# Two graph layers on one core: PSUM pools in another order, one operation for row plus normed row, index work queued later, and both extra weight places opened with the last projection

## The chip, the cores and the metric

The kernel runs on one core of a Trainium2 chip. A core has five engines, each with an instruction stream of its own: TensorE (matrix products; PE in the profile, with its weight loads as PEld), the vector engine (DVE), the scalar engine (ACT), GpSimd (POOL) and SyncE (SP). In this kernel SP issues the loads of weights (and a few small transfers early on); ACT and POOL issue nearly all others. All transfers run on the core's 16 DMA engines. The metric is the device time of one execution in microseconds (us). The times of three runs of the kernel before are 1063.53, 1063.5 and 1066.45 us, the median is 1063.53.

## The reference

The input is 384 nodes with 1024 features and 12288 edges. Layer 0 is graph attention plus a mixing layer plus an expert layer that routes each node to two of eight experts; layer 1 is a graph aggregation plus linear attention plus an expert layer that routes each node to one of eight experts. The change lies from the last projection of layer 1 on; what is computed there is:

```python
x = x + gnn(xn) + mix(xn)                 # mix ends in a projection, a residual, a norm
feats = layernorm(x)
aff = feats @ centroids.T
eid = argmax(aff, axis=1)                 # one expert for each node
xhat = (feats - mean) * rsqrt(var + eps)
for e in range(8):
    h = xhat * gamma[e] + beta[e]
    y = feats + relu(h @ w1[e] + b1[e]) @ w2[e] + b2[e]
    alpha = sigmoid(feats @ centroids[e])
    out = out + mask_e * (alpha * y + (1 - alpha) * feats)
x = x + out
```

Since alpha * feats and (1 - alpha) * feats add up to feats, a node's result is x + feats + alpha * (relu(h @ w1 + b1) @ w2 + b2), all of the one expert of that node.

## The kernel before

**Tiling.** The 384 nodes are three blocks of 128 partitions (`nb`); the 1024 features are eight chunks of 128 (`kc`) or two halves of 512 (`hf`). All numbers are 32-bit floats. A weight place holds 2048 KB (16 KB in each partition): one half of a 1024 x 1024 matrix, or all of one expert's w1 or w2 in layer 1.

**Order.** The kernel is written with a tile framework: pools of tiles with a fixed number of buffers, and a scheduler that orders each engine's instructions by its own estimate and sets the waits. Pools that are closed give their memory to later ones, and the first user of a new tile then waits for the last users of what lay there. `tc.issue_after(i)` queues what is issued inside it, on the engine of `i`, behind `i`.

**Weights.** `load_w` and `load_t` (L104 to L125) take the next place from a list called `ring` and issue the load on SP. The list begins as the pool `w` with three places; layer 0 adds one (`w_top`, L606) and two (`w_more`, L727). `layer1` puts one place of the pool `w_last` in front of the list (`LAST`, L37) when the pool `mid` is closed, just ahead of the last projection; `experts1_sorted` appends one place of the pool `w_end`. So the last stretch runs on eight places, as many as two pairs of experts need. SP works its queue in order: a load whose place isn't free yet holds up all that stand behind it.

**The last projection and the router (`layer1`, L1105 to L1215).** `project` multiplies the attention output with `w_fc` (L1116), `mix_norm` norms it and adds it to `x`. `to_router(nb)` transposes the row block into `xT` (L215, L216), multiplies with the centroids (L1150), takes the moments of the row and norms it twice: the expert input goes to `xn1`, half on DVE and half on ACT (`norm_on_both`), and `norm_on_act` (L186) writes the normed row `ft` on ACT (L190). `to_places(nb)` picks the expert, finds the node's place among that expert's rows (`place`), and scatters the row to `xg` in DRAM (L291 on POOL). POOL then adds `ft` to `x` for the first two blocks (L1186), DVE for the third (L1214). `to_first` builds the first expert pair's rows, transposed, as a product with a one-hot matrix (L1190); `scaled` (L967) applies that pair's gamma and beta, the first half on DVE (L973, L974), the second on ACT (L980), giving `xe0`. Last, ACT computes alpha (`info`), and POOL scatters alpha and node number to `ig` (L291).

**The experts (`experts1_sorted`, L1293 to L1382).** The experts go in four pairs, 64 places for each. For a pair: `rows_of` transposes the loaded rows `xs` (L1317) and scales them into `xeT`; `hidden_of` is the w1 product (L1326), whose result DVE and ACT copy to `hs` (L1329, L1330); `by_feature` transposes it (L1338) and adds the bias with relu, half on DVE (L1346), half on ACT (L1344); `give` is the w2 product (L1357), scaled by alpha on DVE (L1360) and scattered with an addition to `out` (L291). The first pair's rows are `xe0`; the other pairs' rows come back from `xg` (L1308). `inf` (L1367) is alpha and node number by place; `half` (L1372) makes the row numbers for the scatters of it; b2 is gathered by node (L306), and L1374 adds alpha * b2 to `x`, which ACT then stores to `out` (L1376). The scatters into `out` wait for these three stores. PSUM has eight banks: `layer1` has four in the pool `pm` and then four in `px`; `experts1_sorted` opens four for transposes (`ps_t4`), then two for h and two for y.

Of the kernel before, what the change touches and what calls it, by code (L numbers as in the profile page):

```python
# [10 lines left out]
F32 = mybir.dt.float32  # L11
I32 = mybir.dt.int32
AF = mybir.ActivationFunctionType
OP = mybir.AluOpType
# [22 lines left out]
LAST = 1  # L37
# [7 lines left out]
def gps_two_layers(ctx: ExitStack, tc: tile.TileContext, d, out: bass.AP):  # L45
# [140 lines left out]
    def norm_on_act(dst, src, mean, rinv):  # L186

        off = small.tile([P, 1], F32, tag="off", name="off")
        ve.tensor_scalar(off, mean, rinv, -1.0, op0=OP.mult, op1=OP.mult)
        ac.activation(dst, src, AF.Identity, bias=off, scale=rinv)  # L190
# [696 lines left out]
    def experts0_sorted(keep):  # L887

        slots, share = keep["slots"], keep["share"]
        with tc.tile_pool(name="act6", bufs=1) as act, \  # L890
                tc.tile_pool(name="work6", bufs=2) as work, \
                tc.tile_pool(name="ps_t6", bufs=3, space=PSUM) as pt, \
                tc.tile_pool(name="ps_h6", bufs=5, space=PSUM) as ph:
# [73 lines left out]
    def scaled(dst, src, g, es):  # L967

        if g == 0:
# [4 lines left out]
            ve.tensor_tensor(to, to, bt, OP.add)  # L974
            return
# [6 lines left out]
    def layer1(keep=None):  # L982


        with tc.tile_pool(name="act2", bufs=1) as act, \
                tc.tile_pool(name="work3", bufs=2) as work, \
# [5 lines left out]
            ed_w = part.tile([P, NB, N], F32, name="ed_w")  # L992
# [3 lines left out]
            hn = act.tile([P, NB, KC * K2V], F32, tag="rows3", name="hn")  # L996
# [40 lines left out]
            kn = act.tile([P, NB, D], F32, tag="kq", name="kn")  # L1037
# [31 lines left out]
            vn = act.tile([P, NB, KC * K2V], F32, tag="rows3", name="vn")  # L1069
# [6 lines left out]
            kv = part.tile([P, KC, K2V], F32, name="kv")  # L1076
# [11 lines left out]
            qT = act.tile([P, KC, N], F32, tag="kq", name="qT2")  # L1088
# [48 lines left out]
            ft = act.tile([P, NB, KC * K2V], F32, tag="rows3", name="ft4")  # L1137
            xT = act.tile([P, KC, N], F32, tag="kq", name="xT4")
# [5 lines left out]
            def to_router(nb):  # L1144
                mix_norm(nb)
                xs, xb, fb = x[:, nb, :], xn1[:, nb, :], ft[:, nb, :D]
                to_t(pm, xT, xs, nb)
                ps = px.tile([P, HB], F32, tag="x", name="x")
                for kc in range(KC):
                    mm(ps[:, :X], lhsT=xT[:, kc, nb * P:(nb + 1) * P], rhs=cen[:, kc, :],  # L1150
# [13 lines left out]
                norm_on_act(fb, xs, mean, rinv)  # L1164
                sums[nb] = (ps, less, rinv)

            def to_places(nb):
                xb, fb = xn1[:, nb, :], ft[:, nb, :D]
# [15 lines left out]
                if nb < NB - 1:  # L1184
                    with tc.issue_after(last[0].ins):
                        gp.tensor_tensor(x[:, nb, :], x[:, nb, :], fb, OP.add)  # L1186
# [27 lines left out]
            ve.tensor_tensor(x[:, NB - 1, :], x[:, NB - 1, :], ft[:, NB - 1, :D], OP.add)  # L1214
# [78 lines left out]
    def experts1_sorted(xe0):  # L1293

        with tc.tile_pool(name="w_end", bufs=1) as w_end, \
                tc.tile_pool(name="act4", bufs=1) as act, \
# [197 lines left out]
```

## Time and profile before

| | us |
|---|---|
| median of the runs | 1063.53 |
| the profiled execution's own time | 1067.88 |
| its span | 1066.2 |
| TensorE busy | 1017.0 (95%) |
| DVE busy | 350.4 (33%) |
| ACT busy | 269.7 (25%) |
| POOL busy | 321.9 (30%) |
| TensorE busy in the window from 980 to 1000 | 14.78 of 20 |
| end of the last y product | 1057.5 |

The span is what the profiler saw from the first to the last instruction; the execution's own time has 1.7 us around it. In the lines of a timeline the first column is the start, the second the time from the first to the last instruction of a merged group (or the duration of a single one); "x32" counts instructions, and each product of 32-bit floats is recorded as two. The brackets hold the idle time of the engine just before the group, and what ended it. Lines of windows give the length, then each engine's busy time with the count of its instructions, then the granted clock of TensorE (1.00 is full), the mean busy share of the 16 DMA engines, and GB/s.

### The profile page before, as it was taken

Reading aid. Unit: us, or ns where it says so; the run is one execution under the profiler, and the core shown is the slowest. Engines: PE = TensorE matmul, PEld = TensorE weight load, DVE = VectorE, ACT = ScalarE, POOL = GpSimd, SP = SyncE. Lnnn points to the kernel's source line nnn. Section 1 sums busy time; section 2 is a strip of 40 time slices with the busy share of each in tenths; the row PEclk is TensorE's granted clock in tenths of the full one; section 3 lists DMA queues with packets and bytes.
Section 4 is the critical chain, followed back from the end, with each engine's and each line's share of the span. In section 5 each row is a group of like instructions: output and inputs, shape, how many; then the busy total and the mean of one; then the engine's idle time right before and its main releaser. Section 6 shows DMA issues by size and latency. Waiting matters only on the chain. (4 is left out here: it accounts for less than half of the span.)

```text
span 1066.2 us, 9480 instructions
## 1 busy us (share of the span) xinstructions
PE 1017.0 (95%) x3437; PEld 554.8 (52%) x3437; DVE 350.4 (33%) x973; ACT 269.7 (25%) x499; POOL 321.9 (30%) x277
## 2 busy tenths in 40 slices
PE   6999999999999999999998999959999999998895
PEld 4555555544555555544465665424444465555252
DVE  4580000006667766701342110061306000474221
ACT  3111111110876666611131111221302010122120
POOL 2142466566686778500001000130002000013121
PEclk9999999999999999999998999969999999998998
DMA  9939523334425242532365888968522222425994
GB/s 348 401 127 372 146 80 103 135 113 93 77 1 138 22 78 1 159 110 98 113 216 210 300 314 289 393 233 293 197 79 79 79 79 79 158 79 197 388 383 120
DMA packets 69813, 183.35 MB, mean 172 GB/s; under 512 B 21520, under 2 KB 22384, under 8 KB 69504
## 3 DMA queue, kind: packets, MB, share of 16 engines
q1 hardware_dynamic: 40640, 146.01, 38.2%
q0 software_dynamic: 25120, 28.88, 11.6%
q10 hardware_dynamic: 4000, 7.79, 1.9%
q8 instruction: 29, 0.48, 0.2%
q14 instruction: 24, 0.20, 0.1%
HBM read 160.22 MB, written 22.96 MB: 172 GB/s over the span
## 5 line engine op out<-in xcount | busy, mean ns | idle before, releaser
L479 POOL DMA_INDIRECT countd<-seen,cells x96 | 153.2, 1596 | 63.2 <-DMA countd<-seen,cells 38.0
L134 PE MATMUL mm<-xnT,w 128*128 128x384 f32 x512 | 165.7, 486 | 0.0
L665 PE MATMUL mm<-xnT,w 128*128 128x384 f32 x384 | 132.4, 493 | 0.0
L134 PEld LDWEIGHTS mm<-xnT,w 128*128 128x128 f32 x512 | 97.1, 190 | 67.5 <-DVE xnT L216 0.2
L479 POOL DMA_INDIRECT lastd<-typ,cells x96 | 95.1, 991 | 110.0 <-DMA lastd<-typ,cells 70.3
L665 PEld LDWEIGHTS mm<-xnT,w 128*128 128x128 f32 x384 | 70.5, 190 | 56.4 <-issue 13.4
L713 PE MATMUL mm<-w,t 128*128 128x512 f32 x192 | 84.3, 595 | 0.8 <-DVE x L401 0.8
L146 PE MATMUL mm<-w,xnT 128*128 128x512 f32 x192 | 82.8, 592 | 0.0
L134 PE MATMUL mm<-t,w 128*128 128x384 f32 x256 | 82.7, 486 | 0.0
L915 PE MATMUL h<-w,xeT 128*128 128x352 f32 x224 | 68.3, 462 | 0.7 <-DVE xeT L907 0.3
L134 PEld LDWEIGHTS mm<-t,w 128*128 128x128 f32 x256 | 48.6, 190 | 33.9
L146 PEld LDWEIGHTS mm<-w,xnT 128*128 128x128 f32 x192 | 36.3, 190 | 45.5 <-issue 45.5
L713 PEld LDWEIGHTS mm<-w,t 128*128 128x128 f32 x192 | 35.9, 190 | 44.1 <-issue 42.2
L585 DVE TENSOR_TENSOR kind<-last 128x1152 f32<-128x1152 f32 x1 | 1.4, 1359 | 165.3 <-DMA last<-lastd 165.3
L915 PEld LDWEIGHTS h<-w,xeT 128*128 128x128 f32 x224 | 41.9, 190 | 24.4 <-DVE xeT L907 2.4
L291 POOL DMA_INDIRECT xg<-xn,slot x3 | 4.0, 1341 | 140.6 <-DVE xn L1127 135.5
L1011 PE MATMUL mm<-w,xnT 128*128 128x512 f32 x96 | 44.8, 627 | 1.3 <-DVE xnT L216 1.3
L1116 PE MATMUL mm<-w,oT 128*128 128x512 f32 x96 | 42.6, 595 | 0.0
L942 PE MATMUL y<-w,hT 128*128 128x512 f32 (+1 forms) x96 | 41.6, 592 | 0.0
L146 PE MATMUL mm<-w,t 128*128 128x512 f32 x96 | 41.4, 592 | 0.0
L526 ACT ACTIVATE t<-mm,cols 128x384 f32<-128x384 f32 x24 | 13.9, 580 | 106.5 <-PE mm L134 106.5
L1066 POOL TENSOR_TENSOR x<-x,gb 128x1024 f32<-128x1024 f32 x3 | 7.3, 2425 | 101.2 <-DVE x L1065 101.2
(298 smaller groups left out, 1201.6 us busy)
## 6 DMA issues: line engine op xcount, KB each, us to landing
w<-in_w1s SPq DMA_DIRECT2D x16, 1408.0 KB
w<-in_xw SPq DMA_DIRECT2D x8, 2048.0 KB
w<-in_xw2s SPq DMA_DIRECT2D x8, 2048.0 KB
w<-in_w2s SPq DMA_DIRECT2D x8, 1536.0 KB
keys<-keyd POOLq DMA_DIRECT2D x4, 1536.0 KB
xg<-blank SPq DMA_DIRECT2D x12, 512.0 KB
xs<-xg POOLq DMA_DIRECT2D x10, 512.0 KB
w<-in_wk SPq DMA_DIRECT2D x2, 2048.0 KB
```

Source lines behind the costliest of these rows:

```text
L134: mm(ps[:, :N], lhsT=w[:, j, kc, :], rhs=rhs[:, kc, :], start=kc == 0, stop=kc == KC - 1)
L146: mm(ps, lhsT=lhs[:, kc, nb * P:(nb + 1) * P], rhs=w[:, kc, :], start=i == 0 and kc == 0, stop=i == len(pairs) - 1 and kc == KC - 1)
L291: i = gp.indirect_dma_start(rows, bass.IndirectOffsetOnAxis(ap=at, axis=0), src, None, bounds_check=n - 1, oob_is_err=False, compute_op=op)
L479: gp.indirect_dma_start(cells[:, :], bass.IndirectOffsetOnAxis(ap=at[:, i, c:c + 1], axis=0), src[:, c:c + 1], None, bounds_check=N * N + ...
L526: ac.activation(dst[:, ob, :], ps, AF.Identity, bias=cols[:, i, ob:ob + 1], scale=1.0)
L665: mm(ps[:, :N], lhsT=w[:, j, kc, :], rhs=xnT[:, kc, :], start=kc == 0, stop=kc == KC - 1)
L713: mm(pss[hf], lhsT=src[:, kc, nb * P:(nb + 1) * P], rhs=w_out[("mwo", "wo")[part]][hf][:, kc, :], start=part == 0 and kc == 0, stop=part = ...
L915: mm(ag[i][:, :F0], lhsT=xeT[kc // 4][:, kc % 4, :], rhs=w1[kc // 4][:, kc % 4, i * F0:(i + 1) * F0], start=kc == 0, stop=kc == KC - 1)
L942: mm(y, lhsT=hT[:k, e, j, :], rhs=w2[:k, e % 2 * len(K2) + j, :], start=j == 0, stop=j == len(K2) - 1)
L1011: mm(ps, lhsT=xnT[:, kc, nb * P:(nb + 1) * P], rhs=ws[hf][:, kc, :], start=kc == 0, stop=kc == KC - 1)
L1066: gp.tensor_tensor(x[:, b, :], x[:, b, :], gb[:, 1, :], OP.add)
L1116: mm(ps, lhsT=oT[:, kc, nb * P:(nb + 1) * P], rhs=ws[hf][:, kc, :], start=kc == 0, stop=kc == KC - 1)
```

## The change

- The three PSUM pools of `experts1_sorted` are opened in the order h, y, transposes; the two of `experts0_sorted` in the order h, transposes.
- `norm_on_act`, which wrote the normed row into `ft`, becomes `add_normed`: x * (rinv + 1) + off in place, on ACT. `ft` goes, and with it the additions on POOL and DVE.
- `hn`, `kn`, `vn` and `qT` move to the pool `mid`; `kv` shares a buffer with `ed_w`; `xT` becomes a tile of one block from the pool `work`, which gets three buffers.
- `LAST` is 2: both extra places are opened with the last projection; `w_end` goes.
- `half`, the three L1374 and the stores of `out` are queued behind the scaling of pair 1's rows, which are now transposed before the first pair's w2 product; the stores move from ACT's queue to SP's.

```diff
-LAST = 1
+LAST = 2
...
-    def norm_on_act(dst, src, mean, rinv):
+    def add_normed(x, mean, rinv):
         off = small.tile([P, 1], F32, tag="off", name="off")
         ve.tensor_scalar(off, mean, rinv, -1.0, op0=OP.mult, op1=OP.mult)
-        ac.activation(dst, src, AF.Identity, bias=off, scale=rinv)
+        more = small.tile([P, 1], F32, tag="more", name="more")
+        ve.tensor_scalar(more, rinv, 1.0, None, op0=OP.add)
+        ac.activation(x, x, AF.Identity, bias=off, scale=more)
...
-                tc.tile_pool(name="ps_t6", bufs=3, space=PSUM) as pt, \
-                tc.tile_pool(name="ps_h6", bufs=5, space=PSUM) as ph:
+                tc.tile_pool(name="ps_h6", bufs=5, space=PSUM) as ph, \
+                tc.tile_pool(name="ps_t6", bufs=3, space=PSUM) as pt:
...
-                tc.tile_pool(name="work3", bufs=2) as work, \
+                tc.tile_pool(name="work3", bufs=3) as work, \
...
-            hn = act.tile([P, NB, KC * K2V], F32, tag="rows3", name="hn")
+            hn = part.tile([P, NB, KC * K2V], F32, tag="rows3", name="hn")
...
-            kn = act.tile([P, NB, D], F32, tag="kq", name="kn")
+            kn = part.tile([P, NB, D], F32, tag="kq", name="kn")
...
-            kv = part.tile([P, KC, K2V], F32, name="kv")
+            kv = part.tile([P, NB * N], F32, tag="ed", name="kv")[:, :KC * K2V].rearrange("p (k c) -> p k c", c=K2V)
...
-                to_t(pm, xT, xs, nb)
+                xT = work.tile([P, D], F32, tag="xn", name="xT4").rearrange("p (a b) -> p a b", b=P)
+                to_t(pm, xT, xs, 0)
...
-                norm_on_act(fb, xs, mean, rinv)
+                add_normed(xs, mean, rinv)
...
-                if nb < NB - 1:
-                    with tc.issue_after(last[0].ins):
-                        gp.tensor_tensor(x[:, nb, :], x[:, nb, :], fb, OP.add)
...
-            ve.tensor_tensor(x[:, NB - 1, :], x[:, NB - 1, :], ft[:, NB - 1, :D], OP.add)
...
-        with tc.tile_pool(name="w_end", bufs=1) as w_end, \
-                tc.tile_pool(name="act4", bufs=1) as act, \
+        with tc.tile_pool(name="act4", bufs=1) as act, \
                 tc.tile_pool(name="work5", bufs=2) as work, \
-                tc.tile_pool(name="ps_t4", bufs=4, space=PSUM) as pt, \
                 tc.tile_pool(name="ps_h4", bufs=2, space=PSUM) as ph, \
-                tc.tile_pool(name="ps_y4", bufs=2, space=PSUM) as py:
-            ring.append(w_end)
+                tc.tile_pool(name="ps_y4", bufs=2, space=PSUM) as py, \
+                tc.tile_pool(name="ps_t4", bufs=4, space=PSUM) as pt:
...
-                    if hf == 0 and between is not None:
-                        got = rows_of(between)
-                return got if between is not None else None
...
-            for hf in range(2):
-                ve.tensor_scalar(half[:, hf, :], inf[:, :, 1].bitcast(I32), 2.0, float(hf), op0=OP.mult, op1=OP.add)
-            for nb in range(NB):
-                ve.scalar_tensor_tensor(x[:, nb, :], b2[:, nb, :], keep["info"][:, nb, 0:1], x[:, nb, :],
-                                        op0=OP.mult, op1=OP.add)
-                ac.dma_start(out[nb * P:(nb + 1) * P, :], x[:, nb, :])
-            xeT = give(0, by_feature(0, hs), 1)
+            hT = by_feature(0, hs)
+            xeT = rows_of(1)
+            with tc.issue_after(scaled_by[0].ins):
+                for hf in range(2):
+                    ve.tensor_scalar(half[:, hf, :], inf[:, :, 1].bitcast(I32), 2.0, float(hf), op0=OP.mult, op1=OP.add)
+                for nb in range(NB):
+                    ve.scalar_tensor_tensor(x[:, nb, :], b2[:, nb, :], keep["info"][:, nb, 0:1], x[:, nb, :],
+                                            op0=OP.mult, op1=OP.add)
+                    nc.sync.dma_start(out[nb * P:(nb + 1) * P, :], x[:, nb, :])
+            give(0, hT)
```

## The prediction

> **What bounds the kernel now.** TensorE is busy for 1017.0 of 1066.2 us, so I read the timeline of TensorE first, for the places where it waits, and only then what it waits for. The change touches the stretch from the last projection of layer 1 to the end, and there it waits like this:
>
> ```profile
> 975.35 3.47 PE L1190 MATMUL first<-own,xn 128*128 128x128 f32 x16 [1.18 <-DVE slot L1181]
> 981.38 8.78 PE L1326 MATMUL h<-w,xe 128*64 128x512 f32 x32 [2.56 <-ACT xe L980]
> 994.00 0.84 PE L1338 MATMUL t<-ident,hs 128*128 128x128 f32 x4 [3.84 <-issue]
> 1005.53 7.09 PE L1326 MATMUL h<-w,xeT 128*64 128x512 f32 x32 [0.83 <-DVE xeT L974]
> 1045.79 0.84 PE L1338 MATMUL t<-ident,hs 128*128 128x128 f32 x4 [0.59 <-DVE hs L1329]
> 1050.46 7.05 PE L1357 MATMUL y<-w,hT 128*64 128x512 f32 x28 [1.85 <-SPq L1392]
> ```
>
> Call the hidden product of expert pair p h0..h3 (L1326), the output product y0..y3 (L1357), the two w1 loads of a pair A0a, A0b.., the two w2 loads B0a, B0b... h0 starts 2.56 us late and takes 8.78 where h1 takes 7.09; then 3.84 us of nothing; then three even pairs of 16 us; and y3 waits for a weight (its releaser is put down to SP's queue). Now the weight queue (second column: from the first issue to the end of the last of the group) and the 16 DMA engines (windows: PE, PEld, DVE, ACT, POOL busy, clock, DMA share, GB/s):
>
> ```profile
> 963.67 16.37 SPq L123 DMA_DIRECT2D w<-in_xw2s  x2
> 990.19 0.92 SPq L123 DMA_DIRECT2D w<-in_xw  x2
> 1004.73 1.07 SPq L123 DMA_DIRECT2D w<-in_xw2s  x2
> 1012.64 2.71 SPq L123 DMA_DIRECT2D w<-in_xw  x2
> 1021.47 7.84 SPq L123 DMA_DIRECT2D w<-in_xw2s  x2
> ```
>
> ```profile
> 974.00:976.00 2.00, 0.82 (x4) 0.72 (x5) 1.42 (x10) 1.99 (x3) 0.00 (x0) 0.50 0.00 0
> 980.00:982.00 2.00, 0.62 (x4) 0.25 (x6) 0.00 (x0) 1.33 (x5) 1.70 (x4) 0.94 0.66 78
> 982.00:984.00 2.00, 2.00 (x8) 0.68 (x6) 0.00 (x0) 0.00 (x0) 1.07 (x2) 0.50 0.87 252
> 1006.00:1010.00 4.00, 4.00 (x22) 1.42 (x20) 0.14 (x1) 0.53 (x2) 0.00 (x0) 1.00 1.02 419
> 1035.00:1040.00 5.00, 5.00 (x26) 2.32 (x24) 1.50 (x2) 0.00 (x0) 2.14 (x2) 1.00 1.02 410
> ```
>
> B1a goes out at 963.67; B1b, the second of that group, only at about 979.67, since its place lies in memory that L1214 and the row scatters still use. From 982 to 1044 no window has a DMA share below 0.87. So the end is set by the weight stream: it empties at 1050.46, and y3's 7.05 us and the 8.7 us from 1057.52 to 1066.2 follow. TensorE's own work is second, some 2.8 us behind (1.85 and about 0.9 inside y3's first four).
>
> The index work, on the vector engine and GpSimd:
>
> ```profile
> 978.06 1.22 DVE L1214 TENSOR_TENSOR x<-x,ft 128x1024 f32<-128x1024 f32 x1
> 979.20 0.69 DVE L974 TENSOR_TENSOR xe<-xe,gbx 128x512 f32<-128x512 f32 x1
> 993.33 0.24 DVE L1372 TENSOR_SCALAR half<-inf 128x4 int32<-128x4 int32 x2 [13.45 <-DMA b<-in_b,own_e]
> 1002.93 1.28 DVE L1374 SCALAR_TENSOR_TENSOR x<-b,info,x 128x1024 f32<-128x1024 f32 x1 [1.58 <-DMA b<-in_b,own_e]
> ```
>
> ```profile
> 988.19 0.77 POOL L1367 DMA_DIRECT2D inf<-ig x1 [5.12 <-DMA ig<-info,slot]
> 1012.13 1.63 POOL L291 DMA_INDIRECT out<-o,half x1 [19.17 <-DMA out<-x]
> ```
>
> `half` stands before the copy of h0 on the vector engine and waits for `inf`: that is the 3.84 us.
>
> **The change, part by part.** *PSUM order in experts1_sorted.* h0's bank was one of px's, still read by L980 to 981.33; now it is one of pm's, long free, and in the built program h0 waits only for L974; its second half waits for L980 piece by piece. L974 also loses L1214 in front of it: 978.06 + 0.69 = 978.75. h0 starts at 978.9, 2.5 us earlier, with no idle in front, so I take 7.1 us for it (row 1005.53), bound 8.78: it ends at 986.0 instead of 990.16. *PSUM order in experts0_sorted*: no wait of TensorE changes in the built program; 0.
>
> *Row plus normed row in one.* Two POOL additions (2.37 us each, beside the projection) and L1214 go; the ACT operation keeps its 1.23 us; three small vector operations of 0.15 us come. The last stands before the last place, where the vector engine waits 0.68 us for the rank: 0 to 0.15, I take 0.1, on the chain to 975.35.
>
> *Index work later.* `half` and the three L1374 stand behind the scaling of pair 1. The copy of h0 needs no `inf`: the wait becomes 0.6 (row 1045.79), 3.2 us less. Pair 1's eight transposes (1.8 us) move from inside y0 to before it. So y0 starts at 986.0 + 0.6 + 0.9 + 2.0 = 989.5 and ends at 997.3 (7.1 to 8.2 long); h1 starts at 997.4 instead of 1005.53: 8.1 us.
>
> *Two places with the last projection, none at the end.* Eight places as before, but both of the last ones come free when the last L1097 and DVE reader of the middle tiles are done, about 914. The first four loads go out at the same four releases (840.10, 860.70, 886.70, 907.34), then A0a and A0b at about 914 instead of one of them; all are read from 978.9 on, so nothing of that shows. The gain: B1a and B1b now take the two places of w_fc, free at 953.7 and 963.67. B1b leaves the full stretch. *Tiles moved into the middle pool, a third work buffer*: the only wait removed is 0.78 us of POOL at 708, for rows that TensorE reads 30 us later; 0.
>
> *The stores of `out`* move from ACT's queue to SP's, between A2a and A2b. Behind them in SP's line are A2b, B2, A3, B3: each waits until L1374 has run three times, which waits for the third b2 gather.
>
> **The sum.** TensorE alone would gain 8.1 + 2.8 = 10.9 us. It doesn't get it, because the stream binds. From 982 to 1050 the windows carry 24.7 MB, nine of the 2.10 MB loads among it. One of them goes: 2.10 / 0.417 MB per us (windows from 1004 to 1015) = 5.0 us. Against it, nothing but the pair rows can run before A2a: they are issued at 981.4 as before and I let them start at 983, where the stream of before had moved about 0.25 MB already: 0.6 us. The other bound is the stream's start with B1b, about 981.2: 1.8 us. So 3.2 to 5.0, I take 4.4, since the row 980 to 982 has only 78 GB/s at a share of 0.66: the small index scatters hold the engines there, and B1b got little. These scatters now run without a load beside them; `inf` then follows at about 983.5 instead of 988.19 (bound: 988.19), the b2 gathers at 984.5 to 988.
>
> Does SP's line run dry? Pair rows, b2, A2a and the stores are 6.8 MB from 983 on: 16.8 us, to 999.8. A2b goes out behind the third L1374: after pair 1's scaling (990.6), after half and two L1374 and the first half of y0 (994), and after the third gather, about 996 (1.57 MB beside A2a at half the rate), so at 997.8, first bytes 1.6 us later (estimate, from the 963.67 load and its bytes in the window from 964). That fits by 0.4 us. If the third gather takes the 11 us it took in before (991.96 to 1002.93), A2b is at 1000 and 1.7 us are lost: bounds 0 and 1.7, I take 0, since one load competes with it instead of two.
>
> TensorE will wait about 5 us before h3 and 1 to 2 before y3. After 2.56 us of waiting the clock fell to 0.50 and h0 lost 1.7; after 1.85 before y3 it stayed 1.00. A loss in h3 is hidden by y3's wait; in y3 it counts: bounds 0 and 1.7, I take 0, by the row at the same place.
>
> The Trainium skill (TensorE: Matmul & The Clock Gate, section Part 1: The HAM clock gate) speaks against this: an idle window of about 3.4 us halves the clock until about as long a busy one has passed. The two falls in the trace, after 2.56 and 3.84 us, fit such free-running windows; by the rule a longer wait at y3 would cost up to 1.7, an estimate, and the sum would be 2.7 instead of 4.4.
>
> So 4.4 us: span 1061.8, time of the profiled execution 1067.88 - 4.4 = 1063.5. That execution lies 4.35 above the median of the runs, 1063.53; against the median I predict 1059.1.
>
> **Rivals.** *The stream does not bind* outside a profiled execution (the plain runs are 4.35 us faster, which speaks for it; full windows at 410 to 419 speak against): TensorE's 10.9 us come, 1052.6. *The freed load does not shorten the stream*: it starts later by the full 1.8 us and loses 1.7 at A2b, 5.0 - 3.5 = 1.5 us, 1062. *Slower: the stores block SP.* If the third gather lands when it did before, at 1002.93, the third store goes at 1004.3, A2b at 1004.7 instead of 990.7, first bytes at 1006.3 while the stream was empty from 999.8: 6.5 us lost against 4.4 won, 1065.6. It decides from a landing of about 1001 on, and is beyond 0.3% from 1004. For it: a weight load behind a store on one queue is new. Against: two loads and a late `inf` made that landing, and both go.
>
> **How the numbers follow.** 0.3%, 3.2 us, is what a measurement here can tell from no change. Forecast 0.62 (own range 1057 to 1061; 0.54 faster, 0.08 same), stream not binding 0.12 (faster), no shorter stream 0.12 (same), blocked SP 0.14 (0.12 slower, 0.02 same). Faster 0.66, same 0.22, slower 0.12. The range 1054.5 to 1063.5 takes in the forecast, the second rival and the near part of the first, and leaves out 0.08 of the first and 0.12 of the slower one.
>
> **What would show it.** h0 at 979 with no wait, 7.1 long at clock 1.00; the transposes of h0 0.6 us after it; h1 at 997 to 998; B1b at 963.7; `inf` near 983.5; the stores at 993 to 997, A2b right behind; waits of some 5 us before h3 and 1 to 2 before y3; the stream empty near 1046. Wrong if A2b comes after 1001, if a window between 983 and 1040 shows the engines idle, or if y3 starts at half clock.

## The result and the profile after

The changed kernel takes 1065.25 us (median of 14 executions, 1059.32 to 1066.74) beside 1066.53 us for the kernel before (median of 14, 1063.28 to 1069.32). The ratio is 0.9982 with a 95% interval of 0.9968 to 0.9997, a gain of 1.9 us (0.3 to 3.4); the two medians lie 1.3 us apart. Within what a measurement here tells from no change, that is "same". The forecast was 1059.1 with a range of 1054.5 to 1063.5.

The first trace of the changed kernel is of an execution of 1059.32 us, its shortest of all. Its TensorE timeline, to be held against the lines of before (start, length, line, shapes, idle time ahead of it):

```profile
971.30 3.78 PE L1187 MATMUL first<-own,xn 128*128 128x128 f32 x16 [1.38 <-DVE slot L1181]
975.01 8.19 PE L1324 MATMUL h<-w,xe 128*64 128x512 f32 x32
983.76 0.84 PE L1336 MATMUL t<-ident,hs 128*128 128x128 f32 x4 [0.56 <-issue]
992.32 7.04 PE L1324 MATMUL h<-w,xeT 128*64 128x512 f32 x32
...
1029.21 10.09 PE L1324 MATMUL h<-w,xeT 128*64 128x512 f32 x30 [3.05 <-SPq L1390]
...
1040.78 8.27 PE L1355 MATMUL y<-w,hT 128*64 128x512 f32 x32
```

h0 has no wait ahead of it, the 3.84 us behind it are 0.56, and a new wait of 3.05 us stands ahead of most of h3. But the first line alone is 4.05 us earlier than in the first trace of before (975.35), in a part that the change hardly touches. So I measure everything from the start of this product, the third of the tile `first`, called S. The time from S to the end of the span, the end stretch, is 86.3 us in this trace and was 90.85 before: 4.5 us, about what I forecast, and more than the medians show. The queue of weights on SP, where the stores (L1374 here) now stand between A2a and A2b, in the same trace:

```profile
950.57 9.90 SPq L123 DMA_DIRECT2D w<-in_xw2s  x2
983.23 0.37 SPq L123 DMA_DIRECT2D w<-in_xw  x1
987.86 5.79 SPq L1374 DMA_DIRECT2D out<-x  x3
993.74 0.53 SPq L123 DMA_DIRECT2D w<-in_xw  x1
```

B1b is out by 960.5, before the full stretch. A2b goes out at 993.74, which is S + 22.4, and the windows around the danger point (S + 24 to S + 30; DMA share and GB/s are the last two columns) are full:

```profile
995.30:997.30 2.00, 2.00 (x12) 0.72 (x10) 0.00 (x0) 0.00 (x0) 0.00 (x0) 1.00 1.03 416
997.30:999.30 2.00, 2.00 (x11) 0.44 (x7) 0.00 (x0) 0.00 (x0) 0.00 (x0) 1.00 1.02 412
999.30:1001.30 2.00, 2.00 (x17) 1.67 (x16) 1.74 (x4) 1.25 (x4) 1.45 (x1) 1.00 0.99 358
```

Had I stopped here, I would have called the forecast right and the medians noise. The other traces say otherwise.

### The profile page after: what moved, and what is told of

It is laid out like the page before. It is cut to its first block, busy times and chain, and to the rows that moved or that the text cites. A ratio compares the mean times of both kernels' runs of the same rounds, so it can differ in the third digit from the quotient of the medians.

```text
span 1057.6 us, 9480 instructions
## 1 busy us (share of the span) xinstructions
PE 1012.9 (96%) x3437; PEld 551.8 (52%) x3437; DVE 348.5 (33%) x975; ACT 270.2 (26%) x499; POOL 318.4 (30%) x275
## 3 DMA queue, kind: packets, MB, share of 16 engines
q0 software_dynamic: 25120, 28.88, 11.9%
## 5 line engine op out<-in xcount | busy, mean ns | idle before, releaser
L667 PEld LDWEIGHTS mm<-xnT,w 128*128 128x128 f32 x384 | 70.5, 190 | 56.4 <-issue 13.4
L917 PEld LDWEIGHTS h<-w,xeT 128*128 128x128 f32 x224 | 41.9, 190 | 24.5 <-DVE xeT L909 2.5
```

What stands on the lines that cost most here:

```text
L667: mm(ps[:, :N], lhsT=w[:, j, kc, :], rhs=xnT[:, kc, :], start=kc == 0, stop=kc == KC - 1)
L917: mm(ag[i][:, :F0], lhsT=xeT[kc // 4][:, kc % 4, :], rhs=w1[kc // 4][:, kc % 4, i * F0:(i + 1) * F0], start=kc == 0, stop=kc == KC - 1)
```

## The experiments

### More traces of the two kernels

Edit: none. These are further executions of the two kernels.

> The changed kernel once more, for a second trace of it. Its profiled execution so far ended 1.55 us ahead of its own start-of-stretch mark by 86.3 us and was 5.7 us below its median, while before's was 1.4 above. If the stretch from the start of the third `first` product to the end is 86 to 87 again, the change gains 4 us or more at the end and what differs between runs lies in the first 970 us. If it is 88 to 90, the first trace was a lucky one: then the length of the wait ahead of h3 and the windows at half clock behind it vary from run to run, and that is where the gain goes.

(In the first trace the stretch from the mark to the end was 86.3 us.)

> The kernel before once more, for a second trace. Its end stretch, from the start of the third `first` product to the end of the span, was 90.85 us. Theory G (the change gains 3.4 to 4.5 us at the end of every execution, and what hides a part of it in the medians is how the clock's idle windows fall in two earlier places, at 568 and 710 us, that cost 0 to 5.3 us): it is 90 to 92 again. Rival H (the first trace of before had a long end and most executions a shorter one): it is 88 to 89.5.

> The changed kernel a third time. Its end stretch was 86.3 and 87.5 us, in two executions that both lie 4 to 6 us below its median and both lost little at 568 and 710 us. Theory G: 86 to 88 again, and if this execution lies near the median, it is the start of the third `first` product that comes at 974 to 977 instead of 971.3. Rival H: an execution near the median has that start at about 971.4 and an end stretch of 90 or more.

> The kernel before, third trace. In two traces y3's last 28 records took 7.05 us at clock 1.00, behind waits of 1.85 and 2.26 us, and the end stretch was 90.85 and 90.2 us. If y3 at half clock belongs to the changed kernel (its stalls ahead of h3 and y3 are longer), it is 7.05 again and the stretch 90 to 91. If it is a matter of where the clock's windows happen to lie, it may be 8 to 8.8 here too, and the stretch 92.

> The changed kernel, fourth trace. Where h0 runs at full clock (7.1 us), A2a goes out 10.7 us after the start of the third `first` product, ahead of the b2 gathers' bytes, and I expect the third L1372 at 23 to 25 us, A2b at 25, windows with a share below 0.9 between 24 and 30 us, and the end of the stream at 69.5 to 71. Where h0 runs partly at half clock (8.2 us), A2a goes out at 11.9, A2b at 22 to 24, no dry window, and the stream ends at 68 to 69. The end stretch is 18 us more than the stream's end, and 20 where y3 runs at half clock.

Measured: the 12 executions of after_again have a median of 1065.05 us and a ratio to before of 0.9989 (0.9974 to 1.0005), a gain of 1.2 us whose interval takes in zero. The traces follow, with those of the experiments below in the same table. Times are from S, except S, h0 and y3; "last weight" is the start of y3's last 28 records, which the last load (B3b) releases (where no wait is recorded, marked ~, the end of y3 less 7.05 us); "y3" is the length of those 28.

| trace | S | h0 | third L1372/L1374 ends | A2b out | last weight | y3 | end stretch |
|---|---|---|---|---|---|---|---|
| before | 975.35 | 8.78 | 28.9 | with A2a | 75.1 | 7.05 | 90.85 |
| before_again | 974.34 | 10.02 | 27.0 | with A2a | 74.5 | 7.05 | 90.2 |
| before_third | 974.38 | 10.01 | 27.3 | with A2a | 74.4 | 7.05 | 89.9 |
| after | 971.30 | 8.19 | 22.0 | 22.4 | ~70.7 | | 86.3 |
| after_again | 971.42 | 8.17 | 23.1 | 23.6 | 71.9 | 7.05 | 87.5 |
| after_third | 976.00 | 7.09 | 24.7 | 25.1 | 73.9 | 8.75 | 91.3 |
| after_fourth | 975.11 | 7.09 | 25.0 | 25.4 | 72.8 | 7.05 | 88.5 |
| e1_places | 974.42 | 8.78 | 21.0 | with A2a | 72.7 | 7.05 | 88.3 |
| e2_order | 972.95 | 7.09 | 29.8 | 30.2 | 77.8 | 8.75 | 95.0 |
| e6_order_act | 974.68 | 7.09 | 31.2 | with A2a | ~75.3 | | 90.9 |
| e4_act_stores | 975.54 | 7.09 | 24.5 | with A2a | 70.6 | 7.05 | 86.3 |
| e4_again | 975.70 | 7.09 | 24.3 | with A2a | ~70.5 | | 86.2 |
| e8_gather_first | 975.98 | 7.09 | 17.7 | 18.1 | 71.1 | 8.75 | 88.4 |

The mean end stretch is 90.3 us before and 88.4 after: 1.9 us, as the first ratio has it. That the two agree so well is partly luck: of the four executions of the changed kernel two are among its shortest (1059.32 and 1060.68 us), and after_third, at 1068.98, is longer than all others. So neither of my two theories was right as put: the change does not gain 3.4 to 4.5 us in every execution (G), and the first trace of before was no long one (H). The changed kernel's end stretch differs by 5 us between executions, before's by 1. The fourth trace, whose h0 took 7.09 us, came as its expectation has it for A2a (S + 10.7), the third L1372, A2b and the windows (0.61 from S + 24 to S + 26). The third trace shows where the time goes. Its vector engine, with the three L1372 that wait for the gathers of b2:

```profile
994.26 1.29 DVE L1372 SCALAR_TENSOR_TENSOR x<-b,info,x 128x1024 f32<-128x1024 f32 x1 [3.85 <-DMA b<-in_b,own_e]
996.98 1.28 DVE L1372 SCALAR_TENSOR_TENSOR x<-b,info,x 128x1024 f32<-128x1024 f32 x1 [1.43 <-DMA b<-in_b,own_e]
...
999.37 1.28 DVE L1372 SCALAR_TENSOR_TENSOR x<-b,info,x 128x1024 f32<-128x1024 f32 x1 [0.45 <-DMA b<-in_b,own_e]
```

The third gather of b2, which the last of these waits for, was issued at 988.91, 10.5 us earlier. Its line, and below it the same pair in the first trace, 8.1 us apart:

```profile
988.91 1.00 POOL L308 DMA_INDIRECT b<-in_b,own_e  x1 [0.30 <-issue]
```

```profile
983.89 1.00 POOL L308 DMA_INDIRECT b<-in_b,own_e  x1 [0.30 <-issue]
```

```profile
992.00 1.28 DVE L1372 SCALAR_TENSOR_TENSOR x<-b,info,x 128x1024 f32<-128x1024 f32 x1 [1.25 <-DMA b<-in_b,own_e]
```

The SP queue of the third trace, its windows (the clock is the number ahead of the DMA share) and its TensorE timeline:

```profile
986.73 0.37 SPq L123 DMA_DIRECT2D w<-in_xw  x1
995.58 5.44 SPq L1374 DMA_DIRECT2D out<-x  x3
1001.11 1.28 SPq L123 DMA_DIRECT2D w<-in_xw  x1
```

```profile
1000.00:1002.00 2.00, 2.00 (x12) 0.72 (x10) 1.32 (x2) 0.00 (x0) 0.00 (x0) 1.00 0.64 250
1002.00:1004.00 2.00, 2.00 (x16) 1.21 (x12) 0.94 (x2) 0.45 (x2) 0.00 (x0) 1.00 0.76 240
1004.00:1006.00 2.00, 2.00 (x11) 1.00 (x11) 1.60 (x6) 2.00 (x8) 1.09 (x1) 1.00 0.95 332
...
1051.50:1054.50 3.00, 3.00 (x9) 0.88 (x7) 0.00 (x0) 0.00 (x0) 0.00 (x0) 0.50 0.02 5
```

```profile
979.63 7.09 PE L1324 MATMUL h<-w,xe 128*64 128x512 f32 x32
...
1026.99 8.32 PE L1355 MATMUL y<-w,hT 128*64 128x512 f32 x29 [4.05 <-DMA w<-in_xw2s]
...
1049.90 8.75 PE L1355 MATMUL y<-w,hT 128*64 128x512 f32 x28 [2.31 <-SPq L1390]
```

The third store goes at 1001, A2b behind it at 1001.11 (S + 25.1), and the DMA engines run partly dry for 6 us: against 415 GB/s the three windows lack 0.33, 0.35 and 0.17 MB, which is 2.0 us of stream. TensorE then waits 4.05 us in y2 and 2.31 in y3, and y3 falls to half clock on top (0.50 from 1051.5 to 1054.5).

### The places alone, and the order alone

e1_places (the lines of L1293 to L1382 of before that order the index work, and both orders of the PSUM pools, put back):

```diff
-            xeT = rows_of(1)
-            with tc.issue_after(scaled_by[0].ins):
-                for hf in range(2):
...
-                    nc.sync.dma_start(out[nb * P:(nb + 1) * P, :], x[:, nb, :])
-            give(0, hT)
+            for hf in range(2):
...
+                ac.dma_start(out[nb * P:(nb + 1) * P, :], x[:, nb, :])
+            xeT = give(0, by_feature(0, hs), 1)
```

> This kernel keeps the two weight places with the last projection (and the in-place row plus normed row, the tiles in the middle pool), and puts back as before the order of the PSUM pools, the place of half and of the three L1374 in the vector engine's line, the rows of pair 1 between the halves of y0, and the stores of out on ACT's queue. I measure the end stretch from the start of the third `first` product to the end of the span: 90.85 us before, 86.3 after. Theory A (the weight stream sets the end; the freed load shortens it whatever TensorE does earlier): B1b still goes out near 963.7, h0 still takes its old place and half still holds up its copy, y3 still ends the kernel; the stretch is 86 to 87.5, the ratio to before about that of the whole change, 0.998. Rival B (TensorE's earlier start is what gains; the places only keep it from being lost): h0, its copy and h1 stand where they stood before the change, TensorE has no room but the 1.85 us before y3 and 0.9 in it, so the stretch is 88.1 or more, and the gain at most 2.8 us of 90.85.

Measured: ratio 0.9989 (0.9974 to 1.0003), 1064.99 us, end stretch 88.3. Its TensorE timeline:

```profile
980.55 8.78 PE L1324 MATMUL h<-w,xe 128*64 128x512 f32 x32 [2.56 <-ACT xe L981]
...
1034.37 8.78 PE L1324 MATMUL h<-w,xeT 128*64 128x512 f32 x30 [2.64 <-SPq L1390]
...
1047.13 7.05 PE L1355 MATMUL y<-w,hT 128*64 128x512 f32 x28 [0.58 <-SPq L1390]
```

h0 starts and takes what it did before; y3 waits 0.58 us instead of 1.85 to 2.37. The stretch is 2.0 us below the mean of before: rival B's figure, up to 2.8 and no more. But y3 still waits for its weight, so the stream sets the end here too, with TensorE 0.6 us behind it. That weight comes at S + 72.7, 2.1 us later than with the stores on ACT in the changed kernel (below). In e1_places A2a goes out at S + 14.9, since h0 ends later, and with the stores on ACT at S + 10.8; that this makes the difference is a reading and not shown.

The expectation was wrong on `half`. It stands ahead of the copy of h0 as before, but no longer holds it up:

```profile
988.75 0.24 DVE L1370 TENSOR_SCALAR half<-inf 128x4 int32<-128x4 int32 x2 [10.81 <-DMA inf<-ig]
```

It runs at S + 14.3 instead of S + 18.0, since `inf` is issued at S + 8.9 instead of S + 12.8, and the transposes of h0 come 0.61 us behind h0 instead of 3.84. So of the 3.2 us that the prediction gave to the later place of `half`, what e1_places keeps of the change brings nearly all, as long as h0 is as late as before.

e2_order undoes the places alone, e6_order_act in addition puts the stores back on ACT:

```diff
-LAST = 2
+LAST = 1
...
+        with tc.tile_pool(name="w_end", bufs=1) as w_end, \
...
+            ring.append(w_end)
```

> This kernel has all of the change but the two places with the last projection: one place there and one at the end, as before. B1b then waits for the memory of the end place. Theory A (the stream sets the end): h0 and h1 come early as after the change, but the eleven us that TensorE gains turn into waits for weights before y1, h3 or y3; the end stretch is 89 to 91 us (90.85 before), the ratio 0.999 to 1.001. Rival B (TensorE's order gains by itself): the end stretch is 86 to 87.5 as after the whole change, the ratio about 0.998. A third way: the stores on SP's queue delay A2b while the stream is not a load ahead, and the stretch is longer than 91.

> The variant e2_order (all of the change but the two places with the last projection) with the stores of out issued by ACT again. e2_order took 1.0041 of before; in its trace the first row gather of b2 landed late, the third store went out 30.0 us after the start of the third `first` product, A2b at 30.2, and the share of the DMA engines was 0.71 to 0.75 from 28 to 34 us. Theory E (what e2_order lost is SP standing behind the stores, and nothing else of the order loses): A2b goes out by 12 us, no dry windows, the stream carries the same 25.4 MB as before and ends where it ended before, so the end stretch is 89.5 to 91 (90.85 and 90.2 before) and the ratio 0.998 to 1.001. Rival (the order itself loses, by TensorE's waits ahead of y0 or its clock): end stretch 92 to 95, ratio 1.002 or more.

Measured: e2_order 1.0041 (1.0021 to 1.006), 1070.89 us, end stretch 95.0, the third way of its expectation; e6_order_act 1.0003 (0.9987 to 1.0019), 1067.45 us, end stretch 90.9, as theory E has it. Without the places B1b goes out at S + 4.3 as before and its bytes run beside the rows of pair 1 and the gathers of b2; TensorE waits 3.63 and 3.98 us for these rows ahead of y0, and in e2_order SP stands behind the gathers until S + 30.2. The SP queue and the windows of e2_order:

```profile
961.55 16.08 SPq L123 DMA_DIRECT2D w<-in_xw2s  x2
...
998.69 4.43 SPq L1376 DMA_DIRECT2D out<-x  x3
1003.18 1.47 SPq L123 DMA_DIRECT2D w<-in_xw  x1
```

```profile
1002.00:1004.00 2.00, 2.00 (x12) 0.70 (x10) 1.43 (x2) 0.00 (x0) 0.00 (x0) 1.00 0.75 299
1004.00:1006.00 2.00, 2.00 (x10) 0.42 (x6) 0.00 (x0) 0.00 (x0) 0.00 (x0) 1.00 0.79 236
```

With the stores on ACT the loss is gone, and there is no gain either: the stream carries 24.9 MB from S + 4 on, as much as in before (22.8 in the changed kernel), and the last weight comes at S + 75.3. So the stores on SP cost about 4 us there (0.0038 of the time), the order alone gains nothing, and the places alone gain about half of what both do with the stores on ACT (below).

### The stores back on ACT, in the changed kernel

```diff
-                    nc.sync.dma_start(out[nb * P:(nb + 1) * P, :], x[:, nb, :])
+                    ac.dma_start(out[nb * P:(nb + 1) * P, :], x[:, nb, :])
```

> The changed kernel with one part undone: the three stores of out are issued by ACT again and not by SP. Then A2b no longer stands behind the third b2 gather in SP's line. In the traces of the changed kernel A2b went out 22.4 and 23.6 us after the start of the third `first` product, and 25.2 after it in the variant with extra matmuls, where the share of the DMA engines fell to 0.60 in the window from 24 to 26 us. Theory E (how late the third gather lands differs from run to run, and when it is late the stream runs dry behind the stores): A2b goes out at 20 us or earlier, no window between 10 and 66 us has a share below 0.9, the end stretch is 85.5 to 87, and the median of the runs is 0.5 to 1.5 us below that of the changed kernel (1065.1). Rival F (the stores on SP cost nothing): the median is the same as the changed kernel's within 0.5 us. A third way: ACT waits for the gather instead, and its half of the copy of h1 comes late; then a wait shows ahead of the transposes of h1.

> The changed kernel with the stores of out on ACT once more, on the same chip as the other three, for the comparison and for a second trace. Theory E: median 1059.5 to 1061.5, ratio to before 0.993 to 0.995, end stretch 85.5 to 87, A2b within 1 us behind A2a.

Measured on two chips: 0.9936 (0.9915 to 0.9956; 6 executions) and 0.996 (0.9944 to 0.9976; 12 executions). The median over all 18 is 1063.1 us beside 1065.3 over the 28 of the changed kernel: 2.2 us, more than the 0.5 to 1.5 that I expected. e4_again's 1063.26 was above what I expected (1059.5 to 1061.5). SP queue, windows, h3 and y3 of the first:

```profile
986.34 0.92 SPq L123 DMA_DIRECT2D w<-in_xw  x2
```

```profile
1000.00:1002.00 2.00, 2.00 (x12) 0.57 (x8) 0.74 (x2) 0.00 (x0) 0.00 (x0) 1.00 1.02 418
1002.00:1004.00 2.00, 2.00 (x17) 1.46 (x14) 1.33 (x4) 0.84 (x3) 0.00 (x0) 1.00 1.03 412
1004.00:1006.00 2.00, 2.00 (x10) 0.99 (x11) 1.21 (x5) 2.00 (x8) 0.00 (x0) 1.00 1.02 420
```

```profile
1033.75 8.76 PE L1324 MATMUL h<-w,xeT 128*64 128x512 f32 x30 [3.89 <-SPq L1390]
...
1046.12 7.05 PE L1355 MATMUL y<-w,hT 128*64 128x512 f32 x28 [0.20 <-SPq L1390]
```

A2a and A2b go out together, although the third L1372 ends as late (S + 24.5) as in the third trace of the changed kernel. No window is dry, the last weight comes at S + 70.6, and the end stretch is 86.3 and 86.2: 4.1 us below before, in executions that are not especially short. This is about the gain that I forecast for the whole change (4.4). The third way of the expectation, in which ACT is held up instead, does not show: h1's transposes follow without a wait.

### The gathers earlier, the stores still on SP

```diff
-            xss = [None] + [load_rows(pair) for pair in range(1, X // 2)]
-            gp.dma_start(inf, ig.rearrange("(a p) b -> p a b", p=P))
+            xss = [None, load_rows(1)]
             for nb in range(NB):
                 gather(b2[:, nb, :], d["b2"], keep["own_e"][:, nb:nb + 1], X)
+            xss += [load_rows(pair) for pair in range(2, X // 2)]
+            gp.dma_start(inf, ig.rearrange("(a p) b -> p a b", p=P))
```

> The changed kernel, stores of out still on SP, with the three b2 gathers moved ahead in GpSimd's line: behind the rows of pair 1, ahead of the rows of pairs 2 and 3 and of inf. The gathers then start about 3 us earlier, ahead of A2a's bytes, which compete with them. Theory E (the length of SP's stop is set by when the third gather lands): the third L1372 ends 19 to 21 us after the start of the third `first` product instead of 22 to 24.7, A2b goes out at 19.5 to 21.5, the stream doesn't run dry, the end stretch is 86 to 87.5 in nearly every execution, and the median is 2 to 5 us below the changed kernel's 1065.1, near that of the variant with the stores on ACT (1060.4). Rival I (what the variant with ACT gained is that SP's queue is free of stores as such, or that the row scatters are later): the median stays within 1 us of 1065.

Measured: 0.9976 (0.9961 to 0.9991), 1064.52 us. Its SP queue and y3:

```profile
986.80 0.37 SPq L123 DMA_DIRECT2D w<-in_xw  x1
991.29 2.72 SPq L1375 DMA_DIRECT2D out<-x  x3
994.11 0.40 SPq L123 DMA_DIRECT2D w<-in_xw  x1
```

```profile
1047.04 8.75 PE L1355 MATMUL y<-w,hT 128*64 128x512 f32 x28 [2.29 <-SPq L1391]
```

The mechanism came as theory E has it: the third addition of b2 (L1373 here) ends at S + 17.7, A2b goes out at S + 18.1, no window is dry, and the last weight comes at S + 71.1, about as with the stores on ACT (70.6). The time did not: the median is 0.7 us below the changed kernel's 1065.25, where I expected 2 to 5, and that is the figure of rival I. In the trace y3's 28 records took 8.75 us, partly at half clock, behind a wait of 2.29 us, and the end stretch is 88.4. With the stores on ACT TensorE waits longer ahead of h3 (3.89 and 5.06 us, against 1.78 here) and comes to y3 only as its weights do; y3 stayed at full clock in both traces. On the same chip e4_again has 1063.26 us, 1.3 us less, which such a y3 (1.7 us) would account for. Whether it holds for most executions, one trace can't say; rival I is not ruled out.

### The wait ahead of h3 filled with work

e3_warm, in `hidden_of`; the extra results are overwritten:

```diff
+                if pair == X // 2 - 1:
+                    for _ in range(8):
+                        mm(h[:CAP, :], lhsT=ident[:, :CAP], rhs=x[:, 0, :HB], start=True, stop=True)
```

> The changed kernel with eight extra matmuls of 512 columns put ahead of the hidden product of pair 3; they write into its PSUM tile and the product starts over it, so the result is the same. They take about 3.5 us at full clock (16 records of 0.22) and lie in the 3.05 us in which TensorE waited there for a weight. Theory C (the wait halved the clock, and h3 took 10.09 us where it takes 6.7 at full clock, with nothing behind it to hide that): the clock stays 1.00 from 1028 to 1036, h3 takes 6.7 to 7.1, and either the end comes 2.5 to 3.4 us earlier, or y3 waits for its weight, which arrived near 1040, so that 1 to 2 us of it come. Rival D (the half clock there does not come from the wait, or does not matter since the weights of y3 are not there before 1040): the clock falls all the same or the end stretch stays 86.3 within 0.5. The ratio to before is 0.9955 by C and 0.998 by D.

Measured: 0.9965 (0.9948 to 0.9982), 1062.84 us: between C's figure and D's. The extra work took twice what I reckoned (about 6.9 us, see e5_by_expert), so it outlasted the wait. In the trace (S = 976.57, A2b at S + 25.2, end stretch 88.5) y3 finds its weights there and takes 7.67 us at clock 1.00. So theory C doesn't hold as put: in the changed kernel h3's half clock was not what ended it. In the first trace of the changed kernel bytes of the last load still moved when y3 had begun (until 1041.3 in windows of 0.5 us; y3 starts at 1040.78), and y3 took 8.27 us at clock 1.00 for what y0 does in 7.09. Beside after_fourth (A2b at S + 25.4, y3 at full clock, the same end stretch of 88.5) this trace saves nothing. What the extra work can save, as I read it, is the half clock that sometimes follows the wait ahead of y3; that this makes the 2.2 us in the medians isn't shown.

### Each expert's matmuls together

```diff
-                for kc in range(KC):
-                    for r in range(2):
+                for r in range(2):
+                    for kc in range(KC):
```

(and in `give` likewise, over both halves of y).

> The changed kernel with the matmuls of each pair in another order: all of the first expert's, then all of the second's, in the hidden product and over both halves of the output product; the sums are the same. A product can then begin when the first of its two loads is there, and when the last load of the kernel (B3b) lands, 16 of 32 records are left instead of 28 to 32. Theory A (the weight stream ends the kernel in most executions): after the stream's end half of y3 is left, 3.5 us instead of 6.2 to 7.1, so the end stretch is 84 to 85 us and the median falls by 2 to 3.5 us against the changed kernel. Theory C (TensorE's half clock in h3 ends it): h3's first half fills the wait ahead of its second, no full window of idle, the clock stays 1.00 and the gain is of the same size; the two are told apart by the clock in h3 and by whether y3's second half waits. Rival (something else than the last weights sets the end: the scatters of out): the end stretch stays 86 to 88.

Measured: 1.0188 (1.0165 to 1.021), 1086.02 us: a failed experiment. y0 of it and, below, of the changed kernel:

```profile
989.99 11.00 PE L1354 MATMUL y<-w,hT 128*64 128x512 f32 x29
```

```profile
985.41 7.09 PE L1355 MATMUL y<-w,hT 128*64 128x512 f32 x32
```

A record takes 0.22 us while the two experts alternate, and 0.38 to 0.43 when one expert's follow each other. The two write different halves of the output's partitions (0 to 63 and 64 to 127). It does not take a running sum: the extra matmuls of e9_halves_warm (below), which all write one half and add nothing up, take 0.44 each (7.03 us for 16). The Trainium skill (TensorEngine Tiling (Array Packing), Tiling Modes, Key Properties) says that different tiles of the array can execute matmuls in parallel; the two rows agree. The eight products grow by about 4 to 6 us each, TensorE becomes the bound, and the run tells nothing on the stream.

### A version with the last loads in halves

e7_halves (stores on ACT; pair 3's two w2 loads by column halves, first halves first), and e9_halves_warm (ten extra matmuls ahead of h3 in addition):

```diff
+                    for hf in range(2):
+                        for v, e in zip(w2, es):
+                            cs = slice(hf * HB, (hf + 1) * HB)
+                            loads.append(nc.sync.dma_start(v[:, :, cs], d["xw2s"][e].rearrange("c p f -> p c f")[:, :, cs]))
```

> The changed kernel with the stores of out on ACT, and pair 3's two w2 loads cut in halves by column and queued first halves first, so that the first half of y3 needs 2.1 of the last 4.2 MB. This is for a version that beats both kernels. Theory A with C: where the stream is the bound, after its end only half of y3 (3.5 us) is left instead of 6.2, so up to 2.7 us come; where TensorE is the bound (half clock in h3 behind a wait of 3 to 4 us, as in the trace of the variant with the stores on ACT, in which y3 waited only 0.2), nothing comes. Expected: end stretch 84.5 to 86.3, median 1058.5 to 1060.5. Rival: loads cut into rows of 2 KB move slower than those of 4 KB, the stream ends later, and the end stretch is 87 or more.

> The variant e7_halves (stores on ACT, pair 3's w2 in halves) with ten extra matmuls of 512 columns ahead of pair 3's hidden product, which starts over what they write. In e7_halves h3 waited 5.55 us for its second weight and then took 9.81 us at half clock, and y3 waited for nothing. Theory C (the clock after the wait is what is lost there, and TensorE sets that end): the clock stays 1.00 from the extra matmuls to y3's end, h3 takes 7.1 after its last weight, y3 begins 2 to 2.7 us earlier and its second half finds its weights, so the end stretch is 83.8 to 85 (86.5 in e7_halves), the median 1059 to 1060.5 (1062.1), the ratio 0.993 to 0.9945. Rival (the clock falls all the same, or the weights of y3 come too late to use it): the end stretch stays 86 or more and the ratio 0.995 to 0.997.

Measured: e7_halves 0.9958 (0.9941 to 0.9976), 1062.11 us, end stretch 86.5, both a little above the expectation and the stretch just under the 87 of its rival; e9_halves_warm 0.9946 (0.9928 to 0.9964), 1061.02 us, end stretch 84.5. h3 in the first, and the extra matmuls and h3 in the second:

```profile
1032.90 9.81 PE L1324 MATMUL h<-w,xeT 128*64 128x512 f32 x30 [5.55 <-DMA w<-in_xw]
```

```profile
1027.44 7.03 PE L1324 MATMUL h<-x,ident 128*64 128x512 f32 x16
...
1034.37 7.40 PE L1327 MATMUL h<-w,xeT 128*64 128x512 f32 x31
```

Once y3 no longer needs the last load at its start, TensorE sets the end, and there the half clock behind the 5.55 us counts: filled, 2.0 us come in the end stretch, as theory C has it. That is one trace of each; the medians lie 1.1 us apart, on two chips, and that of e9_halves_warm is just above the expected 1059 to 1060.5. Both versions, and e4_act_stores, are faster than before by more than their intervals, and their medians are 2.2 to 4.2 us below the changed kernel's; between the three the intervals don't decide.

## Why the prediction was wrong

**The base: 3.0 us.** I took the median of three runs, 1063.53, and noted that the profiled execution lay 4.35 above it. The runs since put before at 1066.5 to 1067.8 (median of 110: 1066.8); the three were low. Had the 4.4 us been right, 1062.1 would have come. The executions of one kernel spread over 7 us, of which up to 5 arise ahead of S: S lay between 970.9 and 976.6 in seventeen traces. Between the first and the third trace of the changed kernel (4.7 us) most of it comes from two places, the first hidden product of layer 0 at 568 us (2.4 us) and the first product of layer 1 at 711 (1.1 us), which run at half clock for a longer or shorter part. Other traces lose time elsewhere: in e3_warm the product at 568 takes 9.73 us, but TensorE waits 2.94 us behind it. The product at 568 in the first and in the third trace of the changed kernel:

```profile
567.73 9.73 PE L917 MATMUL h<-w,xe 128*128 128x352 f32 x32 [0.68 <-ACT xe L791]
```

```profile
568.48 12.10 PE L917 MATMUL h<-w,xe 128*128 128x352 f32 x32 [0.68 <-ACT xe L791]
```

**The step that failed: SP's line, "I take 0".** I wrote that A2b would go out at 997.8, S + 22.4, that this fits by 0.4 us, and that at worst it is at 1000 and 1.7 us are lost. In the first trace it went out at S + 22.4 to the tenth. In the others it was S + 23.6, 25.1 and 25.4: the third gather landed later than I allowed, and the stream ran dry. I let it land 8 us after its issue (988 to 996). It was issued when I said, at S + 12.6 to 12.9, but L1372 could start on it only 8.1, 9.1, 10.5 and 10.9 us later: in two of four traces nearly the 11 us of before, which I had only as the bound. One load beside the gathers instead of two, my reason for the 0, did bring the third L1372 forward, from S + 27.0 to 28.9 in before, but to 22.0 to 25.0, and I had needed 22. By my own working (dry from S + 24.4, first bytes 1.6 us behind A2b) 25.1 and 25.4 lose 2.3 and 2.6 us: more than my bound, which stopped at a gather of 11 us. Set against the stores on ACT, the last weight comes 0.2, 1.4, 3.4 and 2.3 us later, 1.8 on average; in the medians the stores on SP cost 2.2 us, and about 4 without the places. The rival "the stores block SP" was the right mechanism at a third of its price (6.5 us). I had it as a case of 0.14 beside the forecast, where it belonged into the forecast's sum. Of my signs of being wrong, windows with idle engines behind A2a came in two traces of four (0.64 and 0.61) and y3 at half clock in one; A2b at S + 25.4 would be 1000.8 on the scale of the prediction, just short of the 1001 that I had named.

What made the gathers differ is argued, not shown. In the two traces with the early A2b, h0 ran 8.2 us partly at half clock, and A2a, whose place it frees, went out at S + 11.9. In the two others h0 took the 7.09 that I forecast, A2a went out at S + 10.7, and the gathers landed later beside it. The gain in h0 would then bring the loss. Five variants with A2a at S + 10.7 to 10.8 fit, with the third addition of b2 ended at S + 24.3 to 24.8 (e3_warm, e4_act_stores, e4_again, e7_halves, e9_halves_warm), and so does e1_places (14.9 and 21.0). Against it stands e5_by_expert: A2a at S + 11.8, and still S + 24.6.

**The stream's gain: right.** 4.4 us from the load that leaves the full stretch; with the stores on ACT the last weight is 4.1 us earlier than in before (70.6 beside a mean of 74.7), and so is the end. It needs both parts: 2.0 by the places alone, nothing by the order alone. I had this as "TensorE second, 2.8 us behind". The other two rivals fall with it: the stream does bind, for y3 waits for its last weight in the traces of before and in three of the four of the changed kernel, and the freed load does shorten it, from 24.9 to 22.8 MB.

**TensorE's part: right in kind.** h0 without a wait (S + 3.6 forecast; 3.6 and 3.7 measured) and 7.09 long in two of four traces, the transposes 0.53 to 0.56 us behind it (0.6). h1 came at S + 19.8 to 21.0 instead of 22.1, since eight transposes ahead of y0 took 1.04 us, not 2.0. "A loss in h3 is hidden by y3's wait" held: behind 10.09 us of h3 in the first trace, y3 still began ahead of the last bytes.

**The clock in y3, "I take 0": between the bounds.** Behind waits of 1.9 to 2.4 us, y3's last 28 records took 7.05 us in five traces (three of before, two after) and 8.75 in three (after_third, e2_order, e8_gather_first). The Trainium skill (TensorE: Matmul & The Clock Gate, Part 1: The HAM clock gate) says that the window which halves the clock is free-running, so that equal waits need not cost the same; these rows agree. The figure of that window, about 3.4 us of idling, does not fit them: the waits ahead of the three halvings are 2.29 to 2.33 us, and what else counts no run here shows. The prediction took the fall after 2.56 us ahead of h0 for a fit; that wait is shorter than the window too. In the changed kernel it is one trace of four, 0.4 us on average, which is an estimate.

The sum in traces: 4.1 less 1.8 less 0.4 is 1.9, the 1.9 us of the end stretches. These are the same traces counted in parts, so the sum proves nothing by itself; the gain itself is read from the runs, 1.9 and 1.2 us by their ratios. Half a microsecond more or less in any part can't be told from so few traces. Open stays why e8_gather_first, with the stream nearly as early as in e4_act_stores, gained 0.7 us in the median and not 2.2; its one trace puts it on the clock in y3.

## What to carry to other kernels

A queue that issues in order should not hold anything that waits for a late result ahead of a load that the bound needs: the three stores cost nothing that shows on ACT and took about half the gain on SP. Where a step "fits by 0.4 us", its mean loss is not 0; take a value between the bounds, and ask what else in the change moves the neighbour that it races against. And one trace per kernel is not enough where executions differ by more than the effect: pick a mark just ahead of the change, and compare from there.

## What the runs showed of the hardware

- Matmuls that write the two halves of the output's partitions take 0.22 us a record when they alternate, against 0.38 to 0.44 in a row on one half (y0: 7.09 us for 32 records and 11.00 for 29). And the 28 records that follow the last load take 7.05 us, as long as all 32 of an undisturbed product (7.09); that one expert's were then left without their partners is my reading, not shown.
- Waits of 1.85 to 2.37 us ahead of y3 left the clock at 1.00 in five executions, and waits of 2.29 to 2.33 halved it in three, for 1.7 us. The three are all of versions with the stores on SP, and none is among the three of before; whether it is chance or lies in these versions, eight traces don't decide.
- S, behind 970 us of the same work, spread over 5.7 us (970.88 in e5_by_expert, 976.57 in e3_warm, which differ only behind S), in part by how long single products ran at half clock.
- As the stream of weights ends, its share falls over some 4 us (in e4_act_stores from 0.93 to 0.63 and 0.29 in windows of 2 us) before it is empty; the last load is not spread evenly over the 16 engines to its end.
